# The tail of a fused conv, attention and mixture-of-experts kernel: sums of batch 6 placed behind the scatters of batch 7

## Chip, cores and metric

The kernel runs on one core of one Trainium2 chip. The metric is the device time of one execution in microseconds. The kernel before takes 3097.98 us, the median of three runs (3097.17 to 3100.47). Engines are named as in the profile: PE (matmuls), PEld (its weight loads), DVE, ACT, POOL and SP. SP issues most DMAs, POOL the indirect ones.

## What is computed

The input x has 8 batches of 256 channels by 32 x 32 pixels, so 1024 tokens of 256 numbers a batch. Cut to what matters, the reference is:

```python
x = x + conv_attention(group_norm(x), ...)       # deformable attention, 64 keys, bias by a small MLP
t = to_tokens(x)
u = layer_norm(t)
t = t + sigmoid((u @ q) @ u.T) @ u               # layer 1 attention, 1024 x 1024 a batch
u = layer_norm(t)
probs = softmax(u @ router.T); rw, re = top_k(probs, 2); rw = rw / rw.sum()
out = u
for e in range(8):
    out = out + combine[:, e] * (gelu(u @ w1[e] + b1[e]) @ w2[e] + b2[e])
t = t + out
```

The mixture of experts at the end is what the change is about. Each token goes to two of eight experts, and the two results are added with weights.

## The kernel before, in words

The kernel does not run every expert on every token. It sorts the tokens by expert: `route` (L812) computes for each token and each of its two choices a row `slot` in a table. Sixteen indirect DMAs on POOL, the scatters at L793, write the tokens' rows (`ut`, 128 rows of 1 KB each) to those rows of a DRAM table `xs`. Then `experts` (L911) goes over the table in tiles of 256 rows. Step by step it fetches rows (`xl`, L925), loads the tile's expert weights w1 and w2 with an index read by SP (L931, L932), transposes the rows (`tp`, L985), does the first matmul (`hp`, L966), Gelu (`ht`, L974), the second matmul (`yp`, L945), adds the bias on DVE (`yt`, L950) and stores the tile to a DRAM table `ys` (L951). Batches 0 to 6 give each expert slots in blocks of 128 (two weight sets a round, 12 rounds), batch 7 in blocks of 256 (one set a round, 15 rounds). At last `combine` (L991), which the code calls sums, has 22 steps. It loads rows of the residual `xc` (L1016), gathers each token's two results with 16 indirect DMAs on POOL (`gs`, L1019), adds them on DVE (L1011), transposes (L1002), copies (`ot`, L1004) and stores the output (L1005). A gather needs all tiles of its batch in `ys`.

All of this is written as Python generators, which are advanced in turns. The order in which they are advanced is the program order, and the function `in_order` (L1189 calls it) fixes it on every engine. Only scatters that stand next to each other are free among themselves. In the main loop, 64 turns a batch, batch b's conv attention runs beside batch b-1's layer 1 attention, with the experts and the sums of earlier batches fitted in.

Behind the main loop is the tail (from L1174). What is left there: for batch 7 the rest of its attention (`rest`, L759: softmax, query, attention slots, sorting, scatters), for batch 6 all experts and sums, for batch 5 the end of its sums. The flags `attending` and `sorting` are set by `rest` while it is in these stages. `sorting` goes up together with `attending` for the five sorting steps, and both are down during the scatters. The list `mains` holds the generators of the attention, `mixtures` those of experts, `sums` those of combine. `step` advances the first of a list by one, and `whole` (L1112) advances the experts of one batch by three steps, which is one round:

```python
    def whole():
        of = mixtures[0][0] if mixtures else NB
        for _ in range(3):
            if mixtures and mixtures[0][0] == of:
                step(mixtures)
```

Two kinds of buffers matter below. `low` (L126) takes one of the 12 buffers of pool t2, which xl, xg, ht, yt, gs, xc, ot and others share. `psum` (L129) takes one of 2 PSUM banks. The w1 and w2 pools have two buffers each.

Of the kernel before, what the change touches and what calls it, by code (L numbers as in the profile page):

```python
# [103 lines left out]
def tile_conv_attn_hybrid(ctx: ExitStack, tc: tile.TileContext, x, par, qw, w1, w2_, cst, out):  # L104
    nc = tc.nc
    NB = x.shape[0]
# [36 lines left out]
    attending = sorting = convolving = False  # L143
# [881 lines left out]
    class Side:  # L1025
# [5 lines left out]
        def step(self, both=True):  # L1031
            busy = False
            if self.waiting and not (sorting and self.busy):
                busy = self.busy
                self.busy = next(self.waiting[0], None)
                if self.busy is None:
                    self.waiting.pop(0)
                    self.busy = True
            if self.left and both and not busy:
                self.left = next(self.prep, self) is not self  # L1040
# [23 lines left out]
    mains, mixtures, sums = [], [], []  # L1064
# [22 lines left out]
    def advance(what):  # L1087
        for steps in list(what):
            if next(steps[1], what) is what:
                what.remove(steps)  # L1090
# [21 lines left out]
# [5 lines that stand above are left out]
# [56 lines left out]
            side.finish()  # L1173
    logits(total - 1)  # L1174
    mains.append((b, below))
    n = sorted_ = 0
    while mains:
        advance(mains)
        if sorted_ or not attending and n % 2:
            whole()  # L1180
        sorted_ = sorted_ or sorting
        step(sums)
        n += 1
    while mixtures:
        whole()
        step(sums)
    while sums:
        step(sums)
# [108 lines left out]
```

## Time and profile before

| What | us |
|---|---|
| median of three runs | 3097.98 |
| the profiled execution | 3097.26 |
| its span in the trace | 3095.5 |
| PE busy, sum over the span | 2814.5 |
| POOL busy, sum over the span | 1381.3 |
| softmax and query of batch 7, with five rounds of batch 6 | 2801.0 to 2841.5 |
| its attention slots | 2841.5 to 2889.0 |
| first scatter of batch 7 to its last | 2922.2 to 2980.0 |
| experts of batch 7, from the first fetch | 2981.7 to 3062.6 |
| sums of batch 7 | 3062.6 to 3095.5 |

All times count from the start of the span. The profile's page gives busy time of each engine, the span in 40 slices of 77 us, and the costliest groups of instructions. The trace behind it can be asked for any stretch: busy time by window, instructions in order of time, and what each instruction waited for. In such a line, `xs<-ut,slot` reads output `<-` inputs, and a bracket gives the idle time of the engine ahead of the instruction and what ended it. PE's busy time is modelled at its ends, and a wait for several things is put down to the one that came last.

### The profile page before, as it was taken

What the parts mean: (1) busy time and instruction counts of PE and PEld (TensorE: products, weight loads), DVE (VectorE), ACT (ScalarE), POOL (GpSimd) and SP (SyncE); (2) the same over time, 40 slices, a digit from 0 to 9 for tenths busy, and PEclk for the clock granted to TensorE, in tenths of its full rate; (3) what the DMA queues carried; (4) which work ended last, traced back from release to release, by engine and by line L of the source; (5) the groups of instructions that cost most, each with busy time, mean ns of one, the idle gap of its engine ahead of it and who ended that gap; (6) DMA issues with size and microseconds to landing.
All of it is one profiled execution on the core that took longest, in us unless ns stands there. A gap on an engine that the chain in (4) does not pass through costs nothing. (4 is left out here: it accounts for less than half of the span.)

```text
span 3095.5 us, 51726 instructions
## 1 busy us (share of the span) xinstructions
PE 2814.5 (91%) x19592; PEld 1391.9 (45%) x19592; DVE 1932.1 (62%) x2968; ACT 1872.0 (60%) x2715; POOL 1381.3 (45%) x945
## 2 busy tenths in 40 slices
PE   3889998899999999999999999999999999998845
PEld 2223443344454454544445444544545444446634
DVE  4887668766765677656865667656776565652211
ACT  3676656666666657666676666666566666663211
POOL 2555334643354544545535463545435454451131
PEclk7999999999999999999999999999999999999968
DMA  2321111111373125512364124731256331645556
GB/s 85 106 46 35 22 28 43 47 37 26 99 215 86 45 62 161 180 47 57 88 190 134 48 59 112 210 91 44 63 150 188 91 75 38 188 124 166 169 179 188
DMA packets 428297, 311.22 MB, mean 101 GB/s; under 512 B 284432, under 2 KB 368656, under 8 KB 428048
## 3 DMA queue, kind: packets, MB, share of 16 engines
q1 hardware_dynamic: 415472, 273.14, 31.5%
q0 software_dynamic: 12288, 33.57, 3.5%
q8 instruction: 155, 2.54, 0.3%
q10 hardware_dynamic: 288, 1.20, 0.1%
q14 instruction: 94, 0.77, 0.1%
HBM read 239.93 MB, written 67.90 MB: 99 GB/s over the span
## 5 line engine op out<-in xcount | busy, mean ns | idle before, releaser
L477 POOL TENSOR_TENSOR h<-ta,nb 128x1024 f32<-128x1024 f32 x512 | 980.8, 1918 | 1187.3 <-PE h2p L490 956.0
L490 PE MATMUL h2p<-h,pr__101 64*64 64x512 f32 x8192 | 1011.4, 606 | 59.6 <-DVE h L498 31.4
L496 ACT ACTIVATE h<-h2p,pr__101 128x1024 f32<-128x1024 f32 x512 | 570.4, 1114 | 537.1 <-PE h2p L490 535.6
L498 DVE TENSOR_TENSOR h<-h2p,nc 128x1024 f32<-128x1024 f32 x512 | 625.5, 1222 | 296.6 <-PE h2p L490 283.7
L475 DVE TENSOR_TENSOR h<-ta,still 128x1024 f32<-128x1024 f32 x512 | 620.1, 1211 | 28.8 <-ACT still L464 26.4
L482 ACT ACTIVATE h<-h 128x1024 f32<-128x1024 f32 x512 | 537.7, 1050 | 9.3 <-POOL h L477 9.1
L490 PEld LDWEIGHTS h2p<-h,pr__101 64*64 64x64 f32 x8192 | 254.0, 132 | 575.1 <-issue 286.6
L517 PE MATMUL sim<-h,pr__101 128*32 128x512 f32 x4096 | 493.4, 599 | 0.0
L950 DVE TENSOR_TENSOR yt<-yp,w 128x512 f32<-128x512 f32 x99 | 68.5, 692 | 352.8 <-PE yp L945 312.4
L517 PEld LDWEIGHTS sim<-h,pr__101 128*32 128x32 f32 x4096 | 107.4, 109 | 361.5 <-issue 361.5
L723 PE MATMUL ap<-qt,tn 128*128 128x256 f32 x1024 | 251.0, 389 | 2.5 <-DVE x L745 1.0
L733 PE MATMUL vp<-tt,sg 128*128 128x256 f32 x1024 | 233.0, 381 | 3.5 <-ACT nc L459 3.3
L723 PEld LDWEIGHTS ap<-qt,tn 128*128 128x128 f32 x1024 | 184.9, 190 | 86.2 <-issue 41.7
L945 PE MATMUL yp<-w,ht 128*128 128x256 f32 x792 | 198.0, 394 | 21.4 <-ACT ht L974 8.1
L1019 POOL DMA_INDIRECT gs<-ys,slot x128 | 129.2, 1009 | 192.5 <-DMA xc<-xu 107.3
L966 PE MATMUL hp<-xg,w 128*128 128x128 f32 (+1 forms) x1464 | 202.0, 291 | 12.5 <-ACT xg L987 3.5
L733 PEld LDWEIGHTS vp<-tt,sg 128*128 128x128 f32 x1024 | 193.7, 190 | 36.5 <-ACT nc L459 5.0
L966 PEld LDWEIGHTS hp<-xg,w 128*128 128x128 f32 x1464 | 182.4, 193 | 54.0 <-issue 33.6
L745 DVE TENSOR_TENSOR x<-x,vp 128x512 f32<-128x512 f32 x64 | 44.0, 688 | 237.1 <-PE vp L733 237.1
L974 ACT ACTIVATE ht<-hp,w 128x128 f32<-128x128 f32 (+1 forms) x366 | 108.2, 376 | 133.3 <-PE hp L966 126.3
L741 ACT ACTIVATE sg<-ap 128x512 f32<-128x512 f32 x128 | 76.4, 597 | 160.4 <-PE ap L723 149.8
L945 PEld LDWEIGHTS yp<-w,ht 128*128 128x128 f32 x792 | 144.5, 193 | 56.5 <-ACT ht L974 13.7
(272 smaller groups left out, 2566.1 us busy)
## 6 DMA issues: line engine op xcount, KB each, us to landing
w<-in_w SPq DMA_DIRECT2D x183, 384.0 KB, 3.7
w<-in_w SPq DMA_DIRECT2D x183, 257.0 KB, 3.4
ta<-fd SPq DMA_DIRECT2D x128, 256.0 KB, 4.9
xl<-xs SPq DMA_DIRECT2D x99, 256.0 KB, 3.3
ys<-yt SPq DMA_DIRECT2D x99, 256.0 KB, 2.2
nb<-fd SPq DMA_DIRECT2D x128, 128.0 KB, 4.7
xb<-in_x SPq DMA_DIRECT2D x8, 1024.0 KB, 4.9
x<-in_x SPq DMA_DIRECT2D x8, 1024.0 KB, 7.5
```

What stands on the lines that cost most here:

```text
L475: nc.vector.tensor_tensor(h1, a, b, ALU.max)
L477: nc.gpsimd.tensor_tensor(h1, a, b, ALU.subtract)
L482: nc.scalar.activation(h1, h1, AF.Relu)
L490: nc.tensor.matmul(h2p[gs, r, :], lhsT=par_("w2")[rs, gs], rhs=h1[rs, g].rearrange("p y x -> p (y x)"), start=True, stop=True, tile_positi ...
L496: nc.scalar.activation(h2, h2p, AF.Relu, bias=par_("cb2"))
L498: nc.vector.tensor_tensor(h2.rearrange("p r (y x) -> p r y x", x=W), h2p.rearrange("p r (y x) -> p r y x", x=W), nc_.unsqueeze(3).to_broad ...
L517: nc.tensor.matmul(sim[32 * q : 32 * q + 32, :], lhsT=par_("z3")[:, 15 - m : 47 - m], rhs=h2s[2 * u + q // 2][:, q % 2, :], start=False, s ...
L723: nc.tensor.matmul(ap[:, u, :], lhsT=tn[:, k, m0 : m0 + P], rhs=qt[:, k, quarter(q)], start=(k == 0), stop=(k == 1),)
L733: nc.tensor.matmul(vp[:, i, :], lhsT=sgs[s][:, u, i * P : (i + 1) * P], rhs=tt[:, 2 * todo[n - 2 + s][1] + u, :], start=(s == u == i == 0) ...
L945: nc.tensor.matmul(yp[:, s, :], lhsT=ht[:, f, s * P : (s + 1) * P], rhs=f2[:, s * several // 2, f * C : (f + 1) * C], start=(f == 0), stop ...
L966: nc.tensor.matmul(hp[:, f, us], lhsT=f1[:, u, k * C + f * P : k * C + (f + 1) * P], rhs=xg[:, k, us], start=(k == 0), stop=(k == 1),)
L1019: nc.gpsimd.indirect_dma_start(out=got[m][:, c, :], out_offset=None, in_=yv[:, :], in_offset=bass.IndirectOffsetOnAxis(ap=slot[:, c, m : m ...
```

## The change

It touches only the tail loop, in three places.

- When `whole` is called beside `rest`. Before: on odd n while neither attention nor sorting runs, and on every n after the first sorting step, the scatters included. After: on every n while sorting, on each ninth n (n % 9 == 4) in attention, and on each third n (n % 3 == 1) otherwise, the scatters included.
- Which sums are advanced in that loop. Before: any, so batch 6's start as soon as its experts are through. After: only those of batches below 6.
- The loop over the experts of batch 7 advances the sums by two steps a round in place of one.

No function is new, and no computation is added or taken away.

```diff
     mains.append((b, below))
-    n = sorted_ = 0
+    n = 0
+
+
     while mains:
         advance(mains)
-        if sorted_ or not attending and n % 2:
+        if sorting or (n % 9 == 4 if attending else n % 3 == 1):
             whole()
-        sorted_ = sorted_ or sorting
-        step(sums)
+        if sums and sums[0][0] < NB - 2:
+            step(sums)
         n += 1
     while mixtures:
         whole()
+        step(sums)
         step(sums)
     while sums:
         step(sums)
```

## The prediction

> **What bounds the kernel now.** I read the slices first (PE at 9 tenths nearly everywhere, then 8845 in the last four slices), so the change lies where PE is not full. The windows over the tail come next: one row a stretch, the columns length, busy PE, PEld, DVE, ACT and POOL, granted clock, DMA share, GB/s.
>
> ```profile
> core 0: us, PE busy (x) PEld busy (x) DVE busy (x) ACT busy (x) POOL busy (x), PEclk, DMA share, GB/s
> 2801.00:2841.50 40.50, 33.10 (x179) 25.66 (x179) 14.58 (x40) 17.70 (x36) 6.97 (x8) 0.96 0.77 247
> 2841.50:2889.00 47.50, 45.50 (x218) 38.51 (x218) 7.45 (x23) 15.11 (x28) 6.52 (x9) 1.00 0.20 62
> ...
> 2922.20:2944.20 22.00, 15.51 (x88) 12.18 (x88) 3.54 (x7) 5.48 (x18) 2.97 (x3) 1.00 0.84 275
> 2944.20:2981.70 37.50, 2.73 (x8) 1.37 (x8) 6.35 (x13) 1.17 (x2) 26.51 (x28) 0.52 0.43 140
> 2981.70:2998.00 16.30, 10.49 (x37) 8.10 (x38) 1.08 (x2) 3.04 (x7) 1.80 (x2) 0.63 0.65 205
> 2998.00:3062.60 64.60, 56.36 (x272) 46.64 (x271) 9.83 (x16) 18.05 (x41) 0.00 (x0) 1.00 0.77 233
> 3062.60:3095.50 32.90, 5.42 (x16) 2.74 (x16) 8.13 (x17) 2.34 (x4) 15.34 (x16) 0.54 0.44 136
> ```
>
> The reader is to see the row that begins at 2944.20: 37.5 us in which PE works 2.7 us and only POOL is busy. After it POOL stands at 0.00 for 64.6 us. What POOL does there is in the timeline of POOL (start, length, line, operation, in brackets the idle time and what ended it):
>
> ```profile
> 2922.23 1.05 POOL L793 DMA_INDIRECT xs<-ut,slot  x1 [27.30 <-DVE slot L894]
> 2923.58 0.96 POOL L793 DMA_INDIRECT xs<-ut,slot  x1 [0.30 <-issue]
> 2924.85 0.96 POOL L793 DMA_INDIRECT xs<-ut,slot  x1 [0.30 <-issue]
> 2946.97 0.98 POOL L1019 DMA_INDIRECT gs<-ys,slot  x1 [21.16 <-DMA xc<-xu]
> 2948.26 0.99 POOL L793 DMA_INDIRECT xs<-ut,slot  x1 [0.31 <-issue]
> 2949.55 0.98 POOL L1019 DMA_INDIRECT gs<-ys,slot  x1 [0.30 <-issue]
> ...
> 2979.05 0.97 POOL L793 DMA_INDIRECT xs<-ut,slot  x1 [0.30 <-issue]
> ```
>
> Three scatters of batch 7 (L793) go out at once. The fourth stands behind a gather of batch 6 (L1019), which must have all of batch 6's ys stored; POOL stands still 21.16 us. Then scatter and gather take turns. SP's timeline shows who waits for the last scatter:
>
> ```profile
> 2981.72 0.87 SPq L925 DMA_DIRECT2D xl<-xs  x2
> ```
>
> That is the first fetch of batch 7's expert rows. The chain of waits that ended last runs the same way: SP and w loads to 2941.95, then POOL's gathers and scatters to 2979, then fetch, w, PE. So the tail from 2922 is a chain: scatters, experts of batch 7 (2981.7 to 3062.6), its sums (32.9 us).
>
> **What the Trainium skill says.** Perfetto Trace Analysis, "DMA Instruction — SWDGE (GPSIMD)": a DMA issued by GpSimd sits through its semaphore wait in a wait queue ahead of its run, and its profiled end is the descriptors' end, not the data's. The trace agrees: nothing of POOL runs in the 21.16 us, and a scatter's 0.97 us are followed by a landing at 2.8 us median (2.4 to 4.6 in the tail). DMA: Bandwidth & Descriptors, "Issuing engines are not separate DMA queues": DMAs of POOL and SP run on the same 16 engines. So gathers beside weight loads share; the highest rate here is 308 GB/s at a share of 0.95 (2920 to 2940). TensorE: Matmul & The Clock Gate, "What's actually happening": after about 3.4 us idle PE falls to half clock. The trace grants 0.52 in the idle stretch.
>
> **The change, part by part.** I count iterations n of the tail loop from the code. Softmax and query take n = 0 to 11 (the flag `attending` is still up from the upper half for n = 0, 1), attention 12 to 29, its finishing 30 to 33, sorting 34 to 38, scatters 39 to 54. A call of `whole` is three steps, one round of expert tiles; batch 6 needs 14 calls (12 rounds). Before: n = 3, 5, 7, 9, 11, 31, 33, 35 to 41. After: 4, 7, 10, 13, 22, 31, 34 to 38, 40, 43, 46. So two rounds move from the softmax stretch into attention, and the last nine are as before, but that one goes behind the first sorting step instead of ahead of it. The sums of batch 5 (ended by n = 15) stay.
>
> *1. Scatters.* Before, the last scatter issues at 2979.05 and SP fetches at 2981.72. After, the POOL program has 16 scatters in a row. They need only `slot`, which still stands behind ten rounds on DVE. Last issue: 2922.23 + 15 x 1.28 (the pitch of the first three and of the turns) = 2941.4; landing 4.6 at most: 2946. SP has its own end: the last ys store of batch 6 is issued at 2943.83. Thirteen scatters of 0.131 MB = 1.70 MB more now lie in 2922 to 2944, where the DMA share is 0.84; at 308 GB/s they take 5.5 us, of which 0.16 x 22 = 3.5 fit in the gaps. SP is so free between 2944.2 (no delay) and 2949.7 (all of it). I take 2947.7: **-34 us** (-37 to -32).
>
> *2. PE's clock.* Idle is some 9 us instead of 43; still over 3.4, so the first round is slow as before: 0. The bound is -3.4: the first hp (3.75 for 1.89), yp (2.49 for 1.99), two tp (1.09 for 0.60).
>
> *3. Gathers beside batch 7's experts.* 22 steps, two a call, so 11 to 12 of 17 calls. They bring 16 gathers (2.10 MB), four xc (1.05) and four out (1.05) = 4.2 MB; 0.85 lie there already (two out, three gathers). 3.35 MB at 310 GB/s = 10.8 us of full DMA. Spare: 0.35 x 16.3 = 5.7 in the warm-up, 0.23 x 36 = 8.3 in the next eight rounds, 14.0 together. On average it fits, at a share near 0.95. In bursts it doesn't: a round is 4.7 us, and w2's load takes 5.2 us in the worst (issued 3003.01, yp at 3008.38 after 1.23 us of wait); yp frees the w2 buffer that yp two rounds later needs, so a microsecond on that load costs half of one a round. I take 0.8 us on the load for ten rounds: +4. Two more transposes (L1002) on PE, 0.47 us each by the rounds with (5.18 at 2995) and without (4.65): +1. Buffers of pool t2 (12, now shared by xl, xg, ht, yt and gs, xc, ot): +1. Adds on DVE (0.48 each, DVE at 10 of 65 us), gathers on POOL (idle) and copies on ACT: nothing, PE's matmuls hide them. If that cover goes, 16 x 0.48 = 8. Sum **+6** (0 to +16).
>
> *4. Two rounds into attention.* A round's PE work is yp 1.99, hp 1.95, tp 0.60 = 4.54. Attention has PE at 45.5 of 47.5, so all of it lengthens it; Gelu's table load (1.28 us, and 1.28 back for Sigmoid) holds the second PSUM bank a little: 2 x 5.8 = +11.6. The softmax stretch loses 9.1 of its 33.1 PE us; its chain (softmax, query, statistics, power on POOL behind a gather, which waited 8.7) has then less to hide it, but its DMA, 0.77, is lightened by 3.7 MB: -9.6. Net **+2** (-4 to +9).
>
> *5. Sorting.* The round at 34 follows the first step, so DVE's chain starts some 4 us sooner, but `slot` comes after the tenth round in both: 0.
>
> *6. The last sums* start after batch 7's last ys store as before, batch 6's long done: 0.
>
> Sum: -34 + 0 + 6 + 2 = -26. The profiled execution took 3097.26 us (span 3095.5), 0.7 below the median of 3097.98. 3097.26 - 26 = **3071 us**.
>
> **The rivals.**
> *B, given back in the experts.* Batch 7's rounds fall to the pace of batch 6's DMA-bound ones (hp at 2913.80 and 2937.71, four rounds: 5.98 us). Ten rounds x 1.3 + 1 = +14 in place of +6: 3079. For it: w2's load has no slack. Against: landings there are 3.7 us median at a share of 0.86, no longer than the 3.6 with batch 7.
> *C, slower.* SP is one queue: ys, xl, two w, then out and xc. If xl's buffer comes free only with the landing of the round's own ys (2.9), and out and xc hold SP for their sources in every second round (3.8 and 2.9, halved), w2 is 6.2 us late; halved by the two-round distance, 3.1 a round, 11 rounds, 34: 3097.3 - 34 + 34 + 1 + 2 = 3100. It decides from 2.8 us a round. Against: ahead of xl I count eleven of twelve buffers live, and tp's and yp's releases come before yt.
> *D, attention pays and the softmax stretch gives nothing back.* The chain there is latency, not PE: +12 in place of +2: 3081.
> *E, it doesn't do what it says.* If some gather were still ahead of a scatter: about 3097. Against: the generators run in program order, and the gathers come after all 16.
>
> **How the numbers follow.** Forecast 0.60, B 0.18, D 0.12, C 0.06, E 0.04. The forecast's own terms give 3053 at the very least (-37, -3.4, 0, -4); all at their best together is unlikely, so I start at 3060. Upward the range takes in B and D with the other bounds on top: 3088. Left out is C, E and the extremes. About 0.2% (6 us) is what a measurement of this kernel can tell from no change. Faster by more: forecast, B and D, 0.90; within: E, 0.04; slower: C, 0.06.
>
> **What would show it.** Right, step by step: 16 scatters at a pitch of 1.28 with no gather among them; the first xl of batch 7 at about 2948 (plus the shift of 4); gathers between that and the twelfth call, POOL no longer at 0.00 beside hp of 128x256; rounds of 5.1 to 5.3 us while gathers run and 4.7 after; two hp rounds within attention; last sums 33 us. Wrong: xl of batch 7 after 2955 (SP or the landing, not POOL, held it), rounds over 6 us (B), over 7.5 (C), or `slot` more than 8 us later than 2922 (D).

## The result, and the profile after

The changed kernel takes 3068.14 us, the median of four runs (3064.48 to 3069.56), against 3098.34 of four runs of the kernel before: a ratio of 0.990 (95% interval 0.9883 to 0.9917), 30 us less. The forecast was 3071 in a range of 3060 to 3088. The profiled execution took 3069.3 us with a span of 3067.5, which is 28.0 below the span of before.

First the windows of the changed kernel, cut at the same events as before: softmax and query, attention slots, finishing, sorting, scatters, the start of batch 7's rounds, the rest of them, the last sums. The columns are those of the prediction's first fence.

```profile
2803.40:2837.57 34.17, 28.11 (x124) 20.54 (x123) 13.31 (x38) 15.09 (x29) 7.22 (x8) 0.85 0.65 210
2837.57:2895.65 58.08, 53.95 (x274) 46.11 (x272) 8.84 (x25) 22.79 (x39) 6.52 (x9) 1.00 0.33 100
2895.65:2912.00 16.35, 11.26 (x63) 8.70 (x62) 4.74 (x16) 5.41 (x11) 2.17 (x3) 0.90 0.46 128
2912.00:2929.70 17.70, 14.65 (x102) 13.14 (x101) 6.61 (x28) 5.41 (x18) 0.00 (x0) 1.00 0.86 259
2929.70:2954.80 25.10, 16.07 (x89) 12.03 (x88) 3.54 (x7) 5.63 (x19) 15.47 (x16) 1.00 0.90 311
2954.80:2971.00 16.20, 10.36 (x40) 8.16 (x41) 1.18 (x2) 3.21 (x7) 3.85 (x4) 0.79 0.84 259
2971.00:3036.40 65.40, 57.33 (x278) 46.70 (x276) 15.57 (x29) 19.05 (x42) 11.84 (x12) 1.00 0.86 272
3036.40:3067.50 31.10, 5.43 (x16) 2.74 (x16) 7.85 (x17) 2.34 (x4) 15.28 (x16) 0.55 0.48 144
```

The row of 37.5 us in which PE worked 2.7 us has no counterpart. From the first scatter to batch 7's first fetch there are now 25.1 us, in which PE is busy for 16 and all 16 scatters run. Of POOL's 16 gathers 15 had stood in the idle row; now four are in the row from 2954.80 and 12 in the one from 2971.00, beside PE's 57.3 busy us. The timeline of POOL shows it one by one:

```profile
2929.70 1.05 POOL L793 DMA_INDIRECT xs<-ut,slot  x1 [28.13 <-DVE slot L894]
2931.06 0.98 POOL L793 DMA_INDIRECT xs<-ut,slot  x1 [0.30 <-issue]
...
2947.52 0.96 POOL L793 DMA_INDIRECT xs<-ut,slot  x1 [0.30 <-issue]
2948.78 0.96 POOL L793 DMA_INDIRECT xs<-ut,slot  x1 [0.30 <-issue]
2957.35 0.98 POOL L1019 DMA_INDIRECT gs<-ys,slot  x1 [7.61 <-DMA xl<-xs]
```

No gather stands between two scatters, and the pitch (start to start) is 1.27 us. What ends the stretch is read from SP's timeline:

```profile
2948.69 5.81 SPq L951 DMA_DIRECT2D ys<-yt  x2
2954.81 0.91 SPq L925 DMA_DIRECT2D xl<-xs  x2
```

SP issues the last stores of batch 6 (the two are merged in this line, the second ends at 2954.5), and the fetch follows at once. So the bound is now SP's queue with batch 6's last rounds, and no longer POOL. The scatters' landing (4.9 us median here, 2.5 in the tail before) would have allowed the fetch slightly sooner: the last one landed at 2953.54.

One reading of the profile before needs a word. The bracket of the gather that waited 21.16 us names `xc<-xu`, a row load, and not `ys`. That gather waits for several semaphores, those of the last `ys` stores among them, and the landing of the very last store (issued at 2943.83) isn't in the trace. SP issues the row load right behind that store, at 2944.40, so both tell of the end of batch 6's rounds.

### The profile page after: what moved, and what is told of

It is laid out like the page before. It is cut to its first block, busy times and chain, and to the rows that moved or that the text cites. A ratio compares the mean times of both kernels' runs of the same rounds, so it can differ in the third digit from the quotient of the medians.

```text
span 3067.5 us, 51729 instructions
## 1 busy us (share of the span) xinstructions
PE 2818.7 (92%) x19592; PEld 1393.1 (45%) x19592; DVE 1931.8 (63%) x2968; ACT 1876.7 (61%) x2719; POOL 1381.5 (45%) x945
## 5 line engine op out<-in xcount | busy, mean ns | idle before, releaser
L723 PE MATMUL ap<-qt,tn 128*128 128x256 f32 x1024 | 251.0, 389 | 3.9 <-ACT ht L974 2.4
L733 PE MATMUL vp<-tt,sg 128*128 128x256 f32 x1024 | 233.0, 381 | 3.5 <-ACT nc L459 3.3
L723 PEld LDWEIGHTS ap<-qt,tn 128*128 128x128 f32 x1024 | 184.9, 190 | 88.2 <-issue 42.1
L733 PEld LDWEIGHTS vp<-tt,sg 128*128 128x128 f32 x1024 | 193.6, 190 | 36.6 <-ACT nc L459 5.0
L966 PEld LDWEIGHTS hp<-xg,w 128*128 128x128 f32 x1464 | 181.4, 192 | 53.9 <-issue 34.1
```

Of the source, the lines that this page charges most:

```text
L723: nc.tensor.matmul(ap[:, u, :], lhsT=tn[:, k, m0 : m0 + P], rhs=qt[:, k, quarter(q)], start=(k == 0), stop=(k == 1),)
L733: nc.tensor.matmul(vp[:, i, :], lhsT=sgs[s][:, u, i * P : (i + 1) * P], rhs=tt[:, 2 * todo[n - 2 + s][1] + u, :], start=(s == u == i == 0) ...
L966: nc.tensor.matmul(hp[:, f, us], lhsT=f1[:, u, k * C + f * P : k * C + (f + 1) * P], rhs=xg[:, k, us], start=(k == 0), stop=(k == 1),)
```

## Experiments

Stages are compared by the same events throughout, read from the timelines: from the softmax's first transposes (L558) to the first ap of the second half (L723), to the last vp's end (L733), to the first scatter, to batch 7's first fetch, to its last yt, to the end. All in us:

| kernel | softmax, query | attention | to first scatter | scatter to fetch | rounds | last sums |
|---|---|---|---|---|---|---|
| before | 41.1 | 47.6 | 33.1 | 59.5 | 81.5 | 32.2 |
| before, again | 42.3 | 47.6 | 33.3 | 60.0 | 79.9 | 31.6 |
| changed | 34.7 | 58.2 | 33.9 | 25.1 | 81.7 | 31.0 |
| changed, again | 31.9 | 58.2 | 33.9 | 24.1 | 82.4 | 30.9 |
| sums moved only | 42.4 | 47.6 | 33.4 | 33.7 | 83.3 | 31.4 |
| sums moved only, again | 39.8 | 47.6 | 31.8 | 24.1 | 82.8 | 31.4 |
| tiles moved only | 31.8 | 58.2 | 34.1 | 51.5 | 84.1 | 30.4 |
| one step a round | 32.0 | 58.2 | 33.9 | 35.6 | 80.9 | 31.0 |
| sums last | 30.8 | 58.2 | 34.3 | 35.2 | 83.7 | 43.9 |
| six rounds in softmax | 47.1 | 47.6 | 40.7 | 21.7 | 82.4 | 31.4 |
| three steps | 34.6 | 58.2 | 33.9 | 25.3 | 84.0 | 31.5 |
| four steps | 34.6 | 58.2 | 33.9 | 34.9 | 98.6 | 31.4 |
| four steps, rows early | 34.4 | 58.2 | 33.9 | 24.0 | 86.5 | 31.6 |

**The sums' place alone.** The kernel before, with the two edits on the sums and without the edit on `whole`:

```diff
         sorted_ = sorted_ or sorting
-        step(sums)
+        if sums and sums[0][0] < NB - 2:
+            step(sums)
         n += 1
     while mixtures:
         whole()
         step(sums)
+        step(sums)
```

> Only the sums are moved; batch 6's rounds stay at their iterations of before (five in the softmax stretch, none in attention). Theory A (the gain is the POOL order, and moving two rounds from softmax into attention cost about 4 us of it): slot to first fetch of batch 7 falls from 59.5 us to about 25 as in the changed kernel, softmax and attention stay at 43 and 47.5 us, and the whole is 3098 - 34 = 3064 us, some 4 below the changed kernel. Rival T (the tiles in attention are needed, since the DMA-bound sorting and scatters can't take the load otherwise): slot to fetch 30 us or more, the whole 3072 or above.

Measured: 3077.63 us, a ratio of 0.9915 (0.9901 to 0.9929). The stretch from scatter to fetch fell to 33.7, not 25. By the numbers written down this speaks for T; but three of the kernels below, with the changed kernel's own program up to that fetch, took 35 there as well, so the excess is not the edit's. The same kernel on another chip, further down, took 24.1.

**The tiles' place alone.** The changed kernel, with the sums as before (any batch in the tail loop, one step a round).

> Only batch 6's rounds are moved; its sums start as soon as its rounds are through, one step an iteration, and one step a round later. Theory A: the first gather now comes behind eight scatters instead of three and waits for the last ys of batch 6, so eight scatters alternate with gathers at a pitch of 2.57 us: slot to fetch about 7 + 20 + 25 = 50 us, against 59.5 before and 25 after; with 5 us lost in softmax and attention the whole is 3094 (3090 to 3098). Rival T: the moved rounds bring most of the gain, the whole is 3080 or below.

Measured: 3093.9 us, a ratio of 0.9972 (0.9964 to 0.9981), and 51.5 us from scatter to fetch. The timeline of POOL in this kernel:

```profile
2937.54 0.96 POOL L793 DMA_INDIRECT xs<-ut,slot  x1 [0.31 <-issue]
2958.11 0.99 POOL L1019 DMA_INDIRECT gs<-ys,slot  x1 [19.61 <-DMA xc<-xu]
2959.40 0.99 POOL L793 DMA_INDIRECT xs<-ut,slot  x1 [0.30 <-issue]
```

The first of these is the eighth scatter. The gather behind it waits 19.61 us, and the other eight scatters then take turns with gathers, as theory A had it. The moved tiles alone bring little, and the 8 us that they bring in this stretch (59.5 to 51.5) are POOL's order too: eight scatters stand ahead of the first gather in place of three.

**One step a round.**

```diff
     while mixtures:
         whole()
         step(sums)
-        step(sums)
```

> The changed kernel with one step of the sums a round in place of two. 17 of 23 steps then lie beside batch 7's rounds and six are left ahead of batch 7's sums. Theory A (the DMA of the gathers is hidden in gaps): rounds of batch 7 as in the changed kernel, 81 to 82 us, and up to 4 us more at the end for the six steps: 3068 to 3072. Rival G (the gathers do cost time beside the rounds, and something else made up for it): rounds shorter by 3 us or more.

Measured: 3077.45 us, 0.9921 (0.9906 to 0.9935). Rounds 80.9, as for theory A, and last sums 31.0, with nothing for the six steps that were left over; the whole lies above theory A's figure because the stretch from scatter to fetch took 35.6.

**No sums beside the rounds.** Both steps taken out of the loop, so that batch 6's sums follow batch 7's rounds.

> The changed kernel with no sums of batch 6 beside batch 7's rounds: all of them come after, ahead of batch 7's own. It measures what gathers, row loads and stores cost the rounds. Theory A: the rounds of batch 7 take 80 to 81 us against 81.6 with them (two or three transposes less), and the end grows by the POOL time of 16 gathers, 16 x 1.25 = 20 us, to about 25: the whole is 3088 to 3094. Rival G: the rounds take 76 us or less, since w loads land in 3.6 us again and not in 4.5; the whole is 3083 to 3087.

Measured: 3091.71 us, 0.9964 (0.9951 to 0.9977): the sums' time comes back at the end, though as 12.9 us (43.9 for 31.0) and not as 20 to 25. That the whole lies in theory A's range is therefore luck: the 35.2 us from scatter to fetch made up for it. The rounds took 83.7, longer than with gathers, but 6.62 us of that is one wait of the last Gelu, behind the last hp, for something that the trace doesn't hold (see what stays open). From the first hp of batch 7 to the last one it is 68.0 us (2966.84 to 3034.86), against 70.4 in the changed kernel (2960.85 to 3031.27), 71.3 in its second run and 70.0 and 68.9 in the two of before. These are single profiles, from more than one chip. So gathers, row loads, stores and transposes together cost the rounds some 3 us, of which four transposes are about 2 (a round of the changed kernel takes 5.13 us with one and 4.65 without). Rival G, which gave the rounds 76 us or less, falls.

**Four steps a round**, so the same traffic in half the rounds.

> The changed kernel with four steps of batch 6's sums a round in place of two, so the same 4.2 MB lie in six rounds instead of twelve: 1.05 MB a round beside 1.18 MB of the round's own. Theory A (there is slack, but it is finite: a round can hide w landings up to some 5.2 us): at 310 GB/s such a round needs 7.2 us of DMA and not 4.7, so batch 7's rounds take 5 to 14 us longer than the 81.6 of the changed kernel: 3073 to 3082. Rival H (what the gathers bring never matters to the rounds, whatever the rate): 81 to 83 us, 3067 to 3069.

Measured: 3096.27 us, 0.9973 (0.9962 to 0.9983). Rounds 98.6, above even theory A's 95.6; first to last hp 87.4. And the DMA share in the slow part is only 0.71, so it isn't the rate. The timeline of DVE in this kernel says what it is:

```profile
2988.79 0.48 DVE L1011 SCALAR_TENSOR_TENSOR xc<-gs,weight,xc 128x256 f32<-128x256 f32 x1 [6.62 <-DMA xc<-xu]
2989.19 0.68 DVE L950 TENSOR_TENSOR yt<-yp,w 128x512 f32<-128x512 f32 x1
2989.79 1.39 DVE L1011 SCALAR_TENSOR_TENSOR xc<-gs,weight,xc 128x256 f32<-128x256 f32 x3
2999.87 0.48 DVE L1011 SCALAR_TENSOR_TENSOR xc<-gs,weight,xc 128x256 f32<-128x256 f32 x1 [8.68 <-DMA xc<-xu]
3000.27 0.68 DVE L950 TENSOR_TENSOR yt<-yp,w 128x512 f32<-128x512 f32 x1
```

An add stands three steps behind its row load xc. With four steps a round both lie in one group; the load is the last that SP issues in the round, the add waits for it, and yt of the next round is queued behind the add. SP's ys of that round waits for yt and stands ahead of the next row load. That closes a ring, once a round: the first adds of the four groups start 9.0 to 11.1 us apart.

**Five and six: the ring opened, and a smaller dose.** Row loads one round earlier in the four-step kernel (for batch 6 only), and three steps without that:

```diff
-                if n % 4 == 0:
-                    xc[m // 2] = low("xc")
-                    nc.sync.dma_start(out=xc[m // 2], in_=xu.rearrange("(m p) c -> p m c", p=P)[:, m : m + 2, :])
+                early = 4 if b == NB - 2 else 0
+                for at in ([0] if n == 0 and early else []) + ([n + early] if n % 4 == 0 and n + early < 16 else []):
+                    m_ = at // 2
+                    xc[m_ // 2] = low("xc")
+                    nc.sync.dma_start(out=xc[m_ // 2], in_=xu.rearrange("(m p) c -> p m c", p=P)[:, m_ : m_ + 2, :])
```

> Four steps of batch 6's sums a round, as in the four-step kernel, but each row load xc is issued four steps (one round) earlier; the traffic is the same. In the four-step kernel the rounds took 98.6 us at a DMA share of 0.71, with the first add of a group waiting 6.6 to 8.7 us for its xc and yt behind it on DVE. Theory Q (that wait, queued ahead of yt on DVE, made the loss, not the DMA's rate): rounds 82 to 88 us, the whole 12 us or more below the four-step kernel's 3096. Rival D (the rate of 1.05 MB more a round made it): rounds 94 us or more.

> Three steps a round. Theory Q: an add then comes one round, 4.7 us, behind its row load or a part of a round more, and xc lands 3 to 4 us after an issue that is last in SP's round; so some adds wait, and the rounds take 84 to 90 us, between 82 of two steps and 98.6 of four. Rival D (rate): 0.79 MB more a round, (1.18 + 0.79) / 0.31 = 6.4 us for a round of 4.8 over eight rounds, 13 us: 94 us or more.

Measured: rows early 3073.69 us (0.9916, 0.9899 to 0.9932), rounds 86.5; three steps 3072.97 (0.9913, 0.9896 to 0.9929), rounds 84.0, at the low end of what was expected. (The wholes of these two and of the four-step kernel are from different chips, and some 10 us of their difference lie from scatter to fetch; the rounds are what is compared.) First to last hp, by steps a round: 68.0 with none, 69.4 with one, 70.4 and 71.3 with two, 72.4 with three, 87.4 with four, 75.4 with four and rows early. So with the same four steps the earlier row loads win back 12.0 us: the jump belongs to the ring, and the rate is left with the one to three us a step that the others show. DVE with rows early, after the first group:

```profile
2982.49 0.48 DVE L1011 SCALAR_TENSOR_TENSOR xc<-gs,weight,xc 128x256 f32<-128x256 f32 x1 [3.25 <-DMA gs<-ys,slot]
2982.89 0.68 DVE L950 TENSOR_TENSOR yt<-yp,w 128x512 f32<-128x512 f32 x1
...
2989.61 0.48 DVE L1011 SCALAR_TENSOR_TENSOR xc<-gs,weight,xc 128x256 f32<-128x256 f32 x1 [2.90 <-DMA gs<-ys,slot]
```

The waits for xc are gone there. What is left are waits of about 3 us for gathers, which are the next in line.

**Six rounds in the softmax stretch, none in attention.**

```diff
-        if sorting or (n % 9 == 4 if attending else n % 3 == 1):
+        if sorting or (n == 1 if attending else n % 2):
```

> The changed kernel with no rounds of batch 6 in attention: six of them lie ahead of it (n = 1, 3, 5, 7, 9, 11), two in its finishing (31, 33), five in sorting, one after. Theory A (a round costs 5.3 us in attention, and 3.2 in the softmax stretch, whose waits it fills): softmax 46 us, attention 47.5, slot to fetch 23 to 25 us, bound by the scatters' landing and not by batch 6's rounds: 3061 to 3065. Rival: the softmax stretch with six rounds is bound by its DMA (6 x 1.84 MB at 300 GB/s are 37 us, with the sums of batch 5 on top), grows to 52 us or more, and the whole is 3068 or above.

Measured: 3079.13 us, 0.9911 (0.9896 to 0.9925). The whole misses theory A's 3061 to 3065 and lies where the rival put it, but not for the rival's reason: softmax 47.1 and attention 47.6 are as in theory A, and the rival's DMA bound is not there (share 0.73). It took 40.7 to the first scatter in place of 33.9: with rounds at both 31 and 33 and four in sorting ahead of `slot`, one more stands between attention's end and `slot` than in the changed kernel, which I had left out. The 3.4 us won from scatter to fetch are less than that.

**The changed kernel, sums alone and before, on one chip.**

> The changed kernel once more, on one chip with the two below, to set its stages beside theirs. The kernels with the same program up to the first fetch of batch 7 (one step, four steps, sums last) took 35 us from slot to fetch where the changed kernel's own profile has 25. Theory V (that stretch, three rounds of batch 6 beside 16 scatters, is long or short by the occasion, not by the program): slot to fetch 34 to 36 us here too, 3076 to 3079 us in all. Rival: the program makes it, and it is 25 us again, 3066 to 3069 us.

> Only the sums moved, again. Theory A (moving two rounds from softmax to attention costs 4 us of the gain): 2 to 5 us below the changed kernel on this chip. Rival T (the moved rounds pay): at or above it.

> The kernel before, profiled on the chip of the two above. Theory V: the stretch from slot to the last ys of batch 6, with only three scatters beside it, takes 22 us as in the first profile, since what lengthens it elsewhere is the scatters beside the rounds. Rival: it is longer here as well, by 5 us or more, so the occasion slows DMA as such.

Measured: changed 3068.39 us (ratio 0.9911, 0.9894 to 0.9929), sums alone 3068.53 (0.9906, 0.9889 to 0.9924), before 3096.38 by the median of the timed runs, 3100.18 in the one that was profiled. From scatter to fetch 24.1, 24.1 and 60.0, so V's figure of 34 to 36 fell; yet the same program gave 35 elsewhere, so the rival's "the program makes it" is no answer either. In the kernel before it is 22.0 us from the first scatter to batch 6's last ys store, as V had it (21.6 in the first profile). The whole times of changed and sums alone can't be told apart. In the two profiles sums alone is 5.1 us shorter (3061.69 for 3066.78), as theory A had it, but four of its six runs took 3068 to 3070. The tiles' move neither pays nor costs anything that these runs show in the total. No version beat the changed kernel beyond the intervals; sums alone is as fast with one edit less.

## Why the prediction was right, step by step

*1. Scatters, -34.* 59.5 to 25.1 is -34.4, and 60.0 to 24.1 on one chip -35.9. Which end is late was right too: SP, not the landing. The 2947.7 for the fetch is not what its own working gives: 5.5 us of transfers, less the 3.5 that fit in the gaps, leave 2.0 behind 2944.2, so 2946.2, or -35.5; the first pair is nearer to the one, the second to the other. And the tail's median landing before is 2.5, not 2.8.

*2. Clock, 0.* The first hp of batch 7 still takes 3.75 us; the granted clock over that start is 0.79 for 0.63. First hp and yp, before and then changed:

```profile
2987.98 3.75 PE L966 MATMUL hp<-xg,w 128*128 128x256 f32 x8 [2.05 <-DMA w<-in_w]
...
2992.66 2.49 PE L945 MATMUL yp<-w,ht 128*128 128x256 f32 x8
```

```profile
2960.85 3.75 PE L966 MATMUL hp<-xg,w 128*128 128x256 f32 x8 [1.70 <-DMA w<-in_w]
...
2965.53 2.00 PE L945 MATMUL yp<-w,ht 128*128 128x256 f32 x8 [0.42 <-ACT ht L974]
```

In this pair hp, tp and yp of the start are 0.8 us shorter together in the changed kernel, in the pair on one chip 0.7 longer. So 0 is right on average, and the rounds below hold that much of either sign.

*3. Gathers beside the rounds, +6: too large.* Rounds went from 81.5 to 81.7, and from 79.9 to 82.4; with the start's 0.8 and 0.7 taken out that is some 1 to 2 us. The step that failed is the +4 for w's load: "a microsecond on that load costs half of one a round. I take 0.8 us on the load for ten rounds". The load did land 0.9 later, as the DMA view of the rounds shows (KB each, median us from issue to landing), first before, then changed:

```profile
w<-in_w SPq DMA_DIRECT2D x15, 384.0 KB, 3.6
w<-in_w SPq DMA_DIRECT2D x15, 257.0 KB, 3.5
```

```profile
w<-in_w SPq DMA_DIRECT2D x15, 384.0 KB, 4.5
w<-in_w SPq DMA_DIRECT2D x15, 257.0 KB, 4.5
...
gs<-ys,slot POOLq DMA_INDIRECT x16, 4.7
```

But that cost nothing: yp's waits for w were 1.6 us in all, against 2.4 before (1.5 in both of the pair on one chip). I had taken the load of 5.2 us, on the chain, for the usual case; only one other there (5.1) was like it. In the other rounds of before, from the third on, the yp starts 4.3 to 5.4 us after its load is issued, so at a median of 3.6 there was a slack of 0.7 to 1.8, and most of 0.9 fits into it. Two sums of this step are off without moving it: two stores and three gathers are 0.92 MB, not 0.85, and the two rounds named differ by 0.53, not 0.47. The +1 for buffers was not tested. The wait that does lie close, add behind row load on DVE, I had not named. "Adds on DVE ... nothing" holds because two steps a round put an add one and a half rounds behind its row; four steps show what it costs when that cover is gone, 17 us.

*4. Two rounds into attention, +2.* In the first pair softmax gave back 6.4 and attention took 10.6, +4.2; on one chip -10.4 and +10.6, +0.2. A round in attention costs 5.3 us, 5.8 was forecast. The softmax stretch itself differs by 3 us between runs of one program.

*5. Sorting, 0:* 33.1 to 33.9. *6. Last sums, 0:* 32.2 to 31.0.

Sum of the first pair: -6.4 + 10.6 + 0.8 - 34.4 + 0.2 - 1.2 = -30.4; the tail began 2.4 later in the changed kernel's profile (2802.9 for 2800.4), and so its span is 28.0 shorter. The total is nearer to the forecast than its terms are: gathers came out some 5 lower, attention with softmax 2 higher in that pair, and the tail began later. That these nearly cancel is luck. Rivals B, C and D did not come. The nearest to C is the four-step ring: a wait queued ahead of yt, though on DVE and for a row, not on SP for a buffer. E is excluded by POOL's timeline.

**What stays open.** On two chips the stretch from scatter to fetch took 34 to 36 us where it is 24 to 25 on a third and in the first profile (whose chip isn't recorded), with the same program up to there. There ACT and DVE wait in the middle of the scatters, for something the trace doesn't hold ("remote"), up to 18.7 us at once: here ACT's of one step a round (us in all, times, longest),

```profile
ACT ht L974 <- remote: 9.5, 1, 9.5
```

and SP's register instructions ahead of a w load, min, median and max ns, are at times 700 or 1400 ns long in place of 42; first one step a round, then the changed kernel:

```profile
L932 SPq FUSED_REGOPS  x26: 3/42/1397, 2895.9 to 2952.2; - x26
```

```profile
L932 SPq FUSED_REGOPS  x29: 42/42/42, 2901.2 to 2959.3; - x29
```

The kernel with only two rounds beside its scatters (six in softmax), from one of those two chips, shows no such wait and 21.7 us. In all five profiles with eight scatters or more beside batch 6's rounds on those chips such waits come there, but scatters can't be the whole condition: the last Gelu's wait in the kernel with no sums beside the rounds is of the same kind, and it came some 90 us after the last scatter.

```profile
3040.07 0.84 ACT L974 ACTIVATE ht<-hp,w 128x256 f32<-128x256 f32 x2 [6.62 <-remote]
```

The cause was not found, and whether the recording has a part in it was not tried. By whole times the sums-only kernel gains 24 us on one of the two chips and 28 on the third, and the intervals of the two ratios overlap.

## What to carry to other kernels

When a queue alternates two kinds of work, ask which kind someone is waiting for and whether the other has a wait of its own: one gather with a wait of 21 us ahead of 13 scatters, and the turns after it, cost 34 us, and reordering two generators removed it. Before adding work to a loop, count for each added instruction how far behind its operand's load it stands and what is queued behind it on its engine; that distance, not the DMA's share, decided 12 of the 17 us that four steps a round cost here. A load's slack is read from the time between its issue and its use, its median landing and the waits that name it, not from the slow load that is on the chain.

## What was not expected of the hardware

The scatters kept their pitch of 1.27 us and the rounds went on at a DMA share of 0.90 to 0.91 and 311 to 325 GB/s; the highest rate found before was 308, over 20 us. Median landings went up to 4.9 us for a scatter (2.5 in the tail before). And one stretch of 25 us was 10 us longer in the profiles from two other chips, while the same program's other stages agree within 3.
